# Recommender with GRU and AUGRU: the first 32 pooled features stored and gathered by themselves, and two feature blocks put ahead of the last attention

## The chip, the cores and the metric

The kernel runs on one core of a Trainium2 chip. The metric is the device time of one execution in microseconds (us), as a median over runs. The engines are TensorE (PE, with its weight loads as PEld), VectorE (DVE), ScalarE (ACT), GpSimd (POOL) and SyncE (SP). SP, ACT and POOL issue the DMAs; DMA that gathers rows by an index comes from POOL alone.

## The reference

The model scores 1024 users with a history of 100 items. A GRU runs over the history, an attention network scores each of its states against the candidate item, the scores go through a masked softmax, and the states are pooled with them. Then a second recurrence (AUGRU) runs over the same states, and a small network gives the result.

```python
def gru_step(h, x_t):                                  # 100 steps
    r, z = sigmoid(i_r + h_r), sigmoid(i_z + h_z)
    n = tanh(i_n + r * h_n)
    h_new = (1.0 - z) * n + z * h
keys = swapaxes(gru_seq, 0, 1)
feat = concatenate([keys, q, keys - q, q * keys], axis=-1)
score = mlp(feat, 3 layers, relu)
score = where(mask[:, :, None] == 1, score, -inf)
attn = softmax(score, axis=1)[..., 0]
pooled = einsum('bt,btd->bd', attn, keys)              # 1024 x 128
att_seq = pooled.T[:T]                                 # 100 x 1024

def augru_step(h, (x_t, a_t)):                         # 100 steps
    r = sigmoid([h, x_t] @ aug_Wr.T + aug_br)
    u = sigmoid([h, x_t] @ aug_Wu.T + aug_bu)
    h_hat = tanh([h * r, x_t] @ aug_Wh.T + aug_bh)
    u = a_t[:, None] * u
    h_new = (1.0 - u) * h + u * h_hat
attention_feature = aug_seq at sequential_length - 1
comb = concatenate([user, item, hist_sum, item * hist_sum, attention_feature])
scores = mlp(comb, 3 layers, sigmoid)
```

The weight `a_t` of AUGRU step t is thus feature t of the pooled vector: the first step needs the whole pooling to be done, but of each user only feature 0; step 31 needs feature 31, and the features from 100 on are not used.

## The kernel before, in words

Everything is fp32. The 1024 users lie along the free dimension in two halves of 512 columns, and the 128 features along the partitions. The order of the work is written out by hand: a schedule by hand is kept as it stands in the program, and each engine runs its own instructions in that order. Tiles carry their waits by semaphores.

**GRU steps 0 to 99** (`gru_phase`). A step does, for each half, six products in packed tiles of 128 x 32 weights (line 524), gates on ACT (536, 555, 556) and sums on DVE (544 to 561). The new state is made in a PSUM bank `pi`; DVE multiplies it with the item to `kq` (563), and ACT copies it to SBUF as `hn` (570, `keep`). For half 0 that copy comes after the first gate of half 1, for half 1 in the next step. DVE transposes the state of the step before in blocks of 32 (583) and SP stores it in DRAM as `keys_d`, four steps at a time (597). The attention of a step runs one step later: `attend(t)` on PE (32 packed matmuls, line 688), which needs the banks `pm` of two steps ago to be read; `take(t)` adds the item part on DVE (722) and applies the relu on ACT (727, 729). The layers of the attention network are done as a pipeline over steps, so that `attend(T-1)`, `attend(T)` and `attend(T+1)` remain when the GRU is over. The scores are stored to rows (734), and a softmax over blocks of steps (`ENDS`) runs in `stage`s on DVE (774 to 811) with an exponent on ACT (794). `pool` multiplies states and weights into `pooled` (614 to 625), half 0 on POOL, half 1 partly on DVE.

**The end of the GRU phase** is what the change touches. Six PSUM banks `b[0..5]` are named for what is left: two for the softmax (`e`), one for scratch of the pooling (`kw`), one for scores (`pt`), two for `features` (`f`). `features` are eight blocks of 128 users: the part of the last network that does not need the AUGRU, four inputs by 200 outputs (eight matmuls of 128 x 200, line 655), copied out by ACT (663) and stored by SP a half at a time (665). `some(0, 1)` runs the next part of blocks 0 and 1: called once it issues their matmuls, called again it copies. Between these calls stand the attention steps, the softmax stages, the pooling and `gather_early`, by which POOL fetches key rows for the AUGRU (177). At the end DVE masks the pooled features (967), and they go to DRAM as `pooled_d`, in four parts of 32 features a half: five stores from SP (971), three from ACT (1289).

**The branch.** Three versions of the AUGRU exist, for narrower or wider cuts of the sorted users. Each engine reads which one fits (1342) and branches to it (1343).

**AUGRU** (`augru_phase`). Users are sorted by length, so that the number of columns shrinks over the steps. PE transposes the keys of the first four steps (1070) and ACT copies them (1071); two gates of step 0 are made ahead (1011, 1013). POOL gathers the pooled features in sorted order, 128 users at a time: eight gathers (147) into `att_r`, called `sorted_rows`. Weights for steps 0 and 1 are spread over the partitions by PE (`weight_row`, 1026). For the others, `store_weights` transposes `att_r` on PE (1048), copies it on DVE (1050) and stores it in DRAM (1051), and each step loads its row two steps ahead (`load_att`, 1057). Then come steps 1 to 99, half by half: PE opens the three gates of the next step with its keys (1088) and closes those of this one with the state (1092); ACT applies sigmoid and tanh; DVE does six operations. POOL gathers the key rows of the next block of eight steps, spread over the half-steps (`due`); each gather is preceded by a copy of one column (`pace`, 176), which holds it until DVE's `rest` (1129) of the current half-step.

Of the kernel before, what the change touches and what calls it, by code (L numbers as in the profile page):

```python
# [9 lines left out]
F32 = mybir.dt.float32  # L10
# [9 lines left out]
P = 128  # L20
B = 1024
T = 100
HB = 512
NH = B // HB
NG = B // P
GH = HB // P

R = 32
# [52 lines left out]
def kernel(ctx: ExitStack, tc: tile.TileContext, a: dict, out: bass.AP):  # L81
# [35 lines left out]
    inv_d = dram.tile([B, 2], I32, name="inv_d")  # L117
    over_d = dram.tile([1, 1], I32, name="over_d")
    att_d = [dram.tile([T, HB], F32, name=f"att_d{i}") for i in range(NH)]
    pooled_d = dram.tile([B, P], F32, name="pooled_d")  # L120
    rlen_d = dram.tile([NG, P], F32, name="rlen_d")
    part_d = dram.tile([B, M0], F32, name="part_d")
    early_d = dram.tile([B, 1], F32, name="early_d")
# [32 lines left out]
    def load_rows(q, i, width, tiles):  # L156

        n = READ[q]
        if q < WHOLE:
            r = rows[q, i] = tiles.tile([P, GH, n * P], F32, tag="once", name="rows")  # L160
            for g in range(GH):
                gather(r[:, g, :], keys_d[q], g, i)
                yield
            return

        parts, tag = (2, "kt") if tiles is kx else (1, "rows")
        some = [
            tiles.tile([P, KH // parts, n * R], F32, tag=tag, name="rows") for _ in range(parts)
        ]
        rows[q, i] = some  # L170
        for k in range(-(-width // R)):
            part, at = divmod(k, KH // parts)
            r = some[part]
            if later.get("pace") is not None:

                nc.gpsimd.tensor_copy(r[:, at, 0:1], later["pace"])  # L176
            nc.gpsimd.indirect_dma_start(  # L177
                out=r[:, at, :],
                out_offset=None,
                in_=keys_d[q],  # L180
                in_offset=bass.IndirectOffsetOnAxis(ap=idx_k[:, k, i : i + 1], axis=0),
            )
            yield

    def all_of(steps):
        for _ in steps:
            pass

    def gru_phase(pools):
# [285 lines left out]
        class Half:  # L475
# [37 lines left out]
            def gru(self, t, after_gate, after_sum):  # L513

                x = self.x[t]
                h = self.h[t - 1] if t else hist[:, self.cols]
                hn = hp.tile([P, HB], F32, tag="h", name="hn")
                self.h[t] = hn

                def gate(g, parts):  # L520
                    p = ps.tile([P, HB], F32, tag="g", name=f"ps{g}")
                    for j, (w, v) in enumerate(parts):
                        for q in range(P // R):
                            nc.tensor.matmul(  # L524
                                p[ts(q, R), :],
                                lhsT=w[:, g, ts(q, R)],
                                rhs=v,
                                start=(j == 0),
                                stop=(j == len(parts) - 1),
                            )  # L530
                    return p

                both = ((wih, x), (whh, h)) if t else ((wih, x),)
                pr = gate(0, both)
                r = wp.tile([P, HB], F32, tag="r", name="r")
                nc.scalar.activation(r, pr, AF.Sigmoid, bias=brz[:, 0:1])  # L536
                after_gate()
                if t:
                    ph = gate(2, ((whh, h),))
                pi = gate(2, ((wih, x),))  # L540
                pz = gate(1, both)
                u = wp.tile([P, HB], F32, tag="u", name="u")
                if t:
                    nc.vector.scalar_tensor_tensor(  # L544
                        out=u,
                        in0=ph,
                        scalar=bhh[:, 2:3],
                        in1=r,
                        op0=ALU.add,
                        op1=ALU.mult,  # L550
                    )
                else:
                    nc.vector.tensor_scalar_mul(u, r, bhh[:, 2:3])
                nc.vector.tensor_add(pi, pi, u)  # L554
                nc.scalar.activation(pi, pi, AF.Tanh, bias=bih[:, 2:3])  # L555
                nc.scalar.activation(pz, pz, AF.Sigmoid, bias=brz[:, 1:2])  # L556
                after_sum()
                d = wp.tile([P, HB], F32, tag="d", name="d")
                nc.vector.tensor_sub(d, h, pi)  # L559
                nc.vector.tensor_mul(d, pz, d)  # L560
                nc.vector.tensor_add(pi, pi, d)  # L561
                kq = wp.tile([P, HB], F32, tag="kq", name="kq", bufs=2 * NH)
                nc.vector.tensor_mul(kq, pi, item[:, self.cols])  # L563
                self.first[t] = hn, kq
                self.copy = hn, pi

            def keep(self):

# [334 lines left out]
        all_of(rest)  # L903

        b = [ps.tile([P, HB], F32, tag="g", name="last") for _ in range(6)]
        banks.update(e=[b[0], b[1]], kw=b[3], pt=b[2], f=[b[4], b[5]])

        features = [half.features(g) for half in halves for g in range(GH)]

        def some(*these):  # L910
            for f in these:
                next(features[f])

        gather_early(4)
        halves[1].keep()
        take(T - 2)
        attend(T - 1)
        stage(2)
        weights = soft["e"][0]
        exponents()  # L920
        some(0, 1)
        take(T - 1)
        some(0, 1)
        attend(T)
        some(2)
        for half in halves:
            half.transpose(T - 1)
        stage()
# [8 lines left out]
        halves[1].pool(1, nc.vector)  # L937
        stage()
        take(T)
        some(2)  # L940
        attend(T + 1)
        some(3, 4)
        stage()
        take(T + 1)
        exponents()
        some(3, 4)
        some(5, 6)
        for half in halves:
            half.store((T - 1) // G)
        halves[1].pool(T, nc.vector)  # L950
        stage()
        gather_early(3)
        halves[0].pool(T, nc.gpsimd)
        some(5, 6)
        some(7)
        stage(2)
        exponents()
        some(7)
        stage()
        halves[0].pool(T, nc.gpsimd)  # L960
        halves[1].pool(T, nc.vector)
        all_of(more_early)


        for half in reversed(halves):
            t = blocked(s_bs[NH * (soft["j"] % 2) + half.i])
            nc.vector.tensor_mul(t, later["used"][:, half.ks, :], pooled[:, half.ks, :])
            to = pooled_d[half.cols, :].rearrange("(k r) (p c) -> p r k c", r=R, c=R)
            later["att", half.i] = [(to[p], t[p * R : (p + 1) * R]) for p in range(P // R)]
        for to, t in later["att", 1] + later["att", 0][G - 1 :]:  # L970
            nc.sync.dma_start(out=to, in_=t)

    def augru_phase(pools, widths, alive):
# [43 lines left out]
        def gather_weights(i):  # L1017
            r = wp.tile([P, GH, P], F32, tag="att_r", name="att_r", bufs=2)
            for g in range(GH):
                gather(r[:, g, :], pooled_d, g, i)  # L1020
            return r

        def weight_row(t, i, p):

# [17 lines left out]
            at = att[1, i] = wp.tile([P, HB], F32, name="at", bufs=6)  # L1042
            nc.scalar.copy(at, p)

        def store_weights(i, p):

            for g in range(GH):
                nc.tensor.transpose(p[:, ts(g, P)], sorted_rows[i][:, g, :], ident)
            rows_t = wp.tile([P, HB], F32, tag="att_t", name="att_t", bufs=2)
            nc.vector.tensor_copy(rows_t, p)  # L1050
            nc.sync.dma_start(out=att_d[i], in_=rows_t[:T, :])
            load_att(2, i)

        def load_att(t, i):
            w = widths[t]
# [229 lines left out]
        gates = [first_step(i) for i in range(NH)]  # L1285
        for i in range(NH):
            load_key(1, i, (FREE_BANK, None)[i])
        for to, t in later["att", 0][: G - 1]:
            nc.scalar.dma_start(out=to, in_=t)
        sorted_rows = [gather_weights(i) for i in range(NH)]  # L1290
        for i in range(NH):
            load_key(2, i, (FREE_BANK, None)[i])
        open_gates(1, 1, EARLY_BANKS)
# [5 lines left out]
        first_weights(0, spare)  # L1299
        ahead = load_rows(1, 1, widths[FIRST[1]], kp)  # L1300
        due = spread_over(-(-widths[FIRST[1]] // R), NH * (FIRST[1] - 2))
        jobs, final = [], None
        for t in range(1, T):
            if t + 1 in FIRST[1:-1]:
                all_of(ahead)
                ahead, due = gathers(FIRST.index(t + 1) + 1), spread(FIRST.index(t + 1) + 1)
            for i in range(NH):
                half_step(t, i)
                for _ in range(due.pop(0) if due else 0):
                    next(ahead, None)  # L1310

                for n, job in enumerate(list(jobs)):
                    job[0] += 1
                    if n == 0 and job[0] > 2 * G and next(job[1], job) is job:
                        jobs.remove(job)
            left = alive[t + 1] if t + 1 < T else 0
            for g in range(1, HB // PR):
                if left <= g * PR < alive[t]:
                    jobs.append([0, predict(g)])
                    if left:  # L1320
                        next(jobs[-1][1])
            if t == T - G:
                final = predict(0, last=True)
                next(final)
            if t == HALF_TIME:
                last_places()
# [89 lines left out]
```

## Time and profile before

| what | value |
|---|---|
| median of 3 runs | 2017.64 us (2016.66 to 2018.54) |
| the profiled execution | 2026.01 us |
| its span | 2024.2 us |
| mean granted TensorE clock | 0.994 |
| PE busy | 1995.2 us (99%) |
| DVE busy | 1680.9 us (83%) |
| POOL busy | 1267.8 us (63%) |
| ACT busy | 943.6 us (47%) |
| GRU phase, by the last GRU matmuls | to about 1378 us of the span |
| AUGRU steps 1 to 99 | from about 1433 us of the span to the end |

The profile is of one execution; times in it count from the start of its span. In the page, each row of section 2 cuts the span into 40 slices of 50.6 us. A row of a timeline gives start, duration, engine, line, operation, the tiles and shape, and in brackets how long the engine had been idle before it and what ended that. A table of stretches gives for each the busy time of PE, PEld, DVE, ACT and POOL with the number of instructions, the granted clock, the share of the DMA engines and their rate. Waits, register loads and branches are run by an engine's sequencer; they are marked with a q (PEldq, POOLq) and are not counted as busy.

### The profile page before, as it was taken

The page shows a single profiled execution, that of the slowest core. Times are in us where ns is not written, and L with a number is a line of the kernel's source. Part 1 is how long each engine was busy: PE and PEld are TensorE (multiplying, and loading weights), DVE is VectorE, ACT ScalarE, POOL GpSimd, SP SyncE. Part 2 cuts the span into 40 slices and gives each one's busy share as a digit, 9 for nine tenths or more (in the row PEclk, how much of TensorE's full clock was granted, in tenths as well). Part 3 has the DMA queues.
Part 4 walks back from the last instruction along what each step waited for, and adds up shares of the span by engine and source line. Part 5 has one row for each costly group of instructions (what it writes and reads, how often), then busy time and mean ns, then how long its engine had stood idle before and what let it go on. Part 6 is the DMA issues. An engine that isn't in the chain of part 4 may idle for free.

```text
span 2024.2 us, 41315 instructions
## 1 busy us (share of the span) xinstructions
PE 1995.2 (99%) x15476; PEld 1037.8 (51%) x15476; DVE 1680.9 (83%) x3068; ACT 943.6 (47%) x1708; POOL 1267.8 (63%) x1311
## 2 busy tenths in 40 slices
PE   9999999999999999999999999998999999999998
PEld 2334444444444444444444444444444556678988
DVE  7878998887988887888888888998577777888886
ACT  4444444444445444445444444544334444445555
POOL 0333939569796959595978676998663345453431
PEclk9999999999999999999999999998999999999999
DMA  4443333323344334333432233343443333333332
GB/s 123 97 117 96 101 106 106 105 87 86 105 114 113 106 117 125 100 114 114 123 107 87 84 100 106 91 122 86 132 122 92 92 105 103 97 96 85 92 73 39
DMA packets 241899, 205.81 MB, mean 102 GB/s; under 512 B 59391, under 2 KB 204647, under 8 KB 241687
## 3 DMA queue, kind: packets, MB, share of 16 engines
q1 hardware_dynamic: 227494, 170.04, 30.1%
q0 software_dynamic: 12320, 32.30, 5.7%
q8 instruction: 123, 2.02, 0.4%
q10 hardware_dynamic: 1872, 0.72, 0.1%
q14 instruction: 90, 0.73, 0.1%
HBM read 146.95 MB, written 54.41 MB: 99 GB/s over the span
## 4 chain that ended last, share of the span: by engine, by line
PE 91%; DVE 4%; issue 1%; ACT 1%; POOL 1%; DMA 1%; DVEq 0%; POOLq 0%; ACTq 0%
PE ps L524 48%; PE pm L688 16%; PE ph L1092 5%; PE pr L1092 4%; PE pu L1092 4%; PE ph L1088 4%; PE pr L1088 4%; PE pu L1088 4%; DMA rows<-keys_d,idx_k 1%; POOL pooled L625 0%; POOL kw L624 0%; DVE pu L1116 0%; DVE ps L561 0%; DVE ps L554 0%; DVE d L560 0%
## 5 line engine op out<-in xcount | busy, mean ns | idle before, releaser
L524 PE MATMUL ps<-x,wih 128*32 128x512 f32 x4800 | 723.8, 592 | 0.0
L524 PE MATMUL ps<-hn,whh 128*32 128x512 f32 x4752 | 718.4, 592 | 1.4 <-ACT hn L570 1.4
L524 PEld LDWEIGHTS ps<-x,wih 128*32 128x32 f32 x4800 | 249.7, 110 | 290.1 <-issue 286.9
L524 PEld LDWEIGHTS ps<-hn,whh 128*32 128x32 f32 x4752 | 247.9, 110 | 286.7 <-issue 282.9
L509 POOL TENSOR_TENSOR xm<-x,m 128x512 f32<-128x512 f32 x200 | 234.3, 1172 | 141.7 <-DMA m<-mask_d 141.4
L536 ACT ACTIVATE r<-ps,brz 128x512 f32<-128x512 f32 x200 | 137.5, 687 | 389.2 <-PE ps L524 387.9
L510 POOL TENSOR_TENSOR hist<-hist,xm 128x512 f32<-128x512 f32 x200 | 259.5, 1297 | 15.7
L177 POOL DMA_INDIRECT rows<-keys_d,idx_k x220 | 213.4, 970 | 84.5 <-POOL rows L176 47.6
L625 POOL TENSOR_TENSOR pooled<-pooled,kw 128x512 f32<-128x512 f32 x191 | 245.8, 1287 | 15.0
L624 POOL TENSOR_TENSOR kw<-kt,e 128x512 f32<-128x512 f32 x191 | 205.9, 1078 | 71.0 <-DVE e L797 70.9
L688 PE MATMUL pm<-hn,wk 128*32 128x512 f32 x1200 | 244.6, 594 | 2.2 <-ACT hn L570 2.2
L688 PE MATMUL pm<-kq,wkq 128*32 128x512 f32 x1200 | 244.6, 594 | 0.0
L555 ACT ACTIVATE ps<-ps,bih 128x512 f32<-128x512 f32 x200 | 132.4, 662 | 228.4 <-DVE ps L554 222.6
L1100 ACT ACTIVATE c<-ph,bh 128x96 f32<-128x96 f32 (+41 forms) x198 | 96.4, 487 | 279.3 <-PE ph L1092 247.7
L688 PE MATMUL pm<-mv,w 128*32 128x512 f32 (+1 forms) x808 | 225.2, 596 | 1.0 <-DVE e L778 1.0
L544 DVE SCALAR_TENSOR_TENSOR u<-ps,bhh,r 128x512 f32<-128x512 f32 x198 | 147.5, 745 | 72.4 <-PE ps L524 69.8
L559 DVE TENSOR_TENSOR d<-hn,ps 128x512 f32<-128x512 f32 x198 | 135.9, 687 | 36.0 <-ACT ps L555 35.5
L554 DVE TENSOR_TENSOR ps<-ps,u 128x512 f32<-128x512 f32 x200 | 140.0, 700 | 25.4 <-remote 4.0
L560 DVE TENSOR_TENSOR d<-ps,d 128x512 f32<-128x512 f32 x200 | 138.3, 691 | 26.1 <-ACT ps L556 11.6
L176 POOL COPY rows<-rest 128x1 f32<-128x1 f32 x204 | 38.7, 190 | 192.9 <-DVE rest L1129 189.1
L570 ACT COPY hn<-ps 128x512 f32<-128x512 f32 x200 | 116.5, 582 | 91.9 <-DVE kq L563 91.9
L1116 DVE TENSOR_TENSOR pu<-pu,c 128x96 f32<-128x96 f32 (+41 forms) x197 | 88.1, 447 | 83.7 <-ACT c L1100 73.8
(190 smaller groups left out, 3228.6 us busy)
## 6 DMA issues: line engine op xcount, KB each, us to landing
x<-in_hist_x SPq DMA_DIRECT2D x210, 256.0 KB
keys_d<-kt SPq DMA_DIRECT2D x48, 1024.0 KB
m<-mask_d SPq DMA_DIRECT2D x200, 128.0 KB
rows<-keys_d,idx_k POOLq DMA_INDIRECT x220
s_b<-mv SPq DMA_DIRECT2D x200, 8.0 KB
keys_d<-kt SPq DMA_DIRECT2D x32, 64.0 KB
at<-att_d SPq DMA_DIRECT2D x34, 48.0 KB
mask_i<-in_mask SPq DMA_DIRECT2D x8, 200.0 KB
```

The costliest lines, as they stand in the source:

```text
L177: nc.gpsimd.indirect_dma_start(out=r[:, at, :], out_offset=None, in_=keys_d[q], in_offset=bass.IndirectOffsetOnAxis(ap=idx_k[:, k, i : i + ...
L509: nc.gpsimd.tensor_mul(d, x, m)
L510: nc.gpsimd.tensor_add(acc, acc, d)
L524: nc.tensor.matmul(p[ts(q, R), :], lhsT=w[:, g, ts(q, R)], rhs=v, start=(j == 0), stop=(j == len(parts) - 1),)
L544: nc.vector.scalar_tensor_tensor(out=u, in0=ph, scalar=bhh[:, 2:3], in1=r, op0=ALU.add, op1=ALU.mult,)
L554: nc.vector.tensor_add(pi, pi, u)
L560: nc.vector.tensor_mul(d, pz, d)
L624: eng.tensor_mul(d, k, w)
L625: eng.tensor_add(acc, acc, d)
L688: nc.tensor.matmul(p[i][s, :], lhsT=w[:, s], rhs=v, start=start, stop=stop)
L1088: nc.tensor.matmul(p, lhsT=m[:, 1, :], rhs=k, start=True, stop=False)
L1092: nc.tensor.matmul(p, lhsT=m[:, 0, :], rhs=v, start=False, stop=True)
```

## The change

The tensor `pooled_d` becomes two: features 0 to 31, and the others. Of each half the first 32 features are stored from SP right after the mask of that half; the other three parts of half 1 follow on SP, those of half 0 on ACT. Ahead of the AUGRU, POOL gathers only the first 32 features. The others are gathered one a half-step from step 5 on (eight gathers, each with a copy for the pace), and transposed and stored as weights of steps 32 to 99 in step 12. The last two key-row gathers of `rows[1, 0]` move from the end of the GRU phase to behind the gathers of weights. In the list of the last attention, feature blocks 0 and 1 come ahead of `take(T - 2)` and `attend(T - 1)`, and the other blocks each move up; the six banks are given out in another order. In the last GRU step the copy of half 1's state comes ahead of `kq` and no longer after it.

```diff
-    pooled_d = dram.tile([B, P], F32, name="pooled_d")
+    pooled_d = [
+        dram.tile([B, n], F32, name=f"pooled_d{j}") for j, n in enumerate((R, P - R))
+    ]
...
+                self.copy = hn, pi
+                if t == T - 1 and self.i:
+                    self.keep()
                 kq = wp.tile([P, HB], F32, tag="kq", name="kq", bufs=2 * NH)
                 nc.vector.tensor_mul(kq, pi, item[:, self.cols])
                 self.first[t] = hn, kq
-                self.copy = hn, pi
...
-        banks.update(e=[b[0], b[1]], kw=b[3], pt=b[2], f=[b[4], b[5]])
+        banks.update(e=[b[0], b[5]], kw=b[4], pt=b[3], f=[b[1], b[2]])
...
         gather_early(4)
-        halves[1].keep()
+        some(0, 1)
         take(T - 2)
         attend(T - 1)
         stage(2)
         weights = soft["e"][0]
         exponents()
         some(0, 1)
+        some(2, 3)
         take(T - 1)
-        some(0, 1)
+        some(2, 3)
         attend(T)
-        some(2)
+        some(4)
...
         take(T)
-        some(2)
+        some(4)
         attend(T + 1)
-        some(3, 4)
+        some(5, 6)
         stage()
         take(T + 1)
         exponents()
-        some(3, 4)
         some(5, 6)
+        some(7)
         for half in halves:
             half.store((T - 1) // G)
         halves[1].pool(T, nc.vector)
         stage()
         gather_early(3)
         halves[0].pool(T, nc.gpsimd)
-        some(5, 6)
         some(7)
         stage(2)
         exponents()
-        some(7)
         stage()
         halves[0].pool(T, nc.gpsimd)
         halves[1].pool(T, nc.vector)
-        all_of(more_early)
+        gather_early(3)
...
-            to = pooled_d[half.cols, :].rearrange("(k r) (p c) -> p r k c", r=R, c=R)
-            later["att", half.i] = [(to[p], t[p * R : (p + 1) * R]) for p in range(P // R)]
-        for to, t in later["att", 1] + later["att", 0][G - 1 :]:
+            first, others = (
+                d[half.cols, :].rearrange("(k r) (p c) -> p r k c", r=R, c=R) for d in pooled_d
+            )
+            nc.sync.dma_start(out=first[0], in_=t[:R])
+            later["att", half.i] = [
+                (others[p - 1], t[p * R : (p + 1) * R]) for p in range(1, P // R)
+            ]
+        for to, t in later["att", 1]:
             nc.sync.dma_start(out=to, in_=t)
...
-                gather(r[:, g, :], pooled_d, g, i)
+                gather(r[:, g, :R], pooled_d[0], g, i)
             return r
+
+        def gather_more():
+            for i in range(NH):
+                for g in range(GH):
+                    r = sorted_rows[i][:, g, R:]
+                    nc.gpsimd.tensor_copy(r[:, 0:1], later["pace"])
+                    gather(r, pooled_d[1], g, i)
+                    yield
...
-        def store_weights(i, p):
-
+        def store_weights(i, p, t0=0, t1=R):
+
+            n = t1 - t0
             for g in range(GH):
-                nc.tensor.transpose(p[:, ts(g, P)], sorted_rows[i][:, g, :], ident)
+                nc.tensor.transpose(p[:n, ts(g, P)], sorted_rows[i][:, g, t0:t1], ident)
             rows_t = wp.tile([P, HB], F32, tag="att_t", name="att_t", bufs=2)
-            nc.vector.tensor_copy(rows_t, p)
-            nc.sync.dma_start(out=att_d[i], in_=rows_t[:T, :])
-            load_att(2, i)
+            nc.vector.tensor_copy(rows_t[:n, :], p[:n, :])
+            nc.sync.dma_start(out=att_d[i][t0:t1], in_=rows_t[:n, :])
+            if t0 == 0:
+                load_att(2, i)
...
-        for to, t in later["att", 0][: G - 1]:
+        for to, t in later["att", 0]:
             nc.scalar.dma_start(out=to, in_=t)
         sorted_rows = [gather_weights(i) for i in range(NH)]
+        for k in range(14, KH):
+            load_row(1, 0, k)
...
+        more = gather_more()
...
             for i in range(NH):
                 half_step(t, i)
                 for _ in range(due.pop(0) if due else 0):
                     next(ahead, None)
+                if t > FIRST[1]:
+                    next(more, None)
+                if t == FIRST[2]:
+                    store_weights(i, pa.tile([P, HB], F32, tag="a", name="pw"), R, T)
```

`FIRST[1]` is 4 and `FIRST[2]` is 12, `R` is 32, `KH` is 16. `load_row(q, i, k)` is the body of the loop in `load_rows`, as a function of its own.

More of the change, by code (lines that the diff above doesn't have):

```diff
@@ L171, in load_rows, with load_row @@
         for k in range(-(-width // R)):
[L172 to L182, printed above, removed]
-            yield
+            load_row(q, i, k)
+            yield
+    def load_row(q, i, k):
+        some = rows[q, i]
+        part, at = divmod(k, KH // len(some))
+        r = some[part]
+        if later.get("pace") is not None:
+            nc.gpsimd.tensor_copy(r[:, at, 0:1], later["pace"])
+        nc.gpsimd.indirect_dma_start(
+            out=r[:, at, :],
+            out_offset=None,
+            in_=keys_d[q],
+            in_offset=bass.IndirectOffsetOnAxis(ap=idx_k[:, k, i : i + 1], axis=0),
+        )
     def all_of(steps):
@@ L967, in gru_phase @@
             nc.vector.tensor_mul(t, later["used"][:, half.ks, :], pooled[:, half.ks, :])
-            to = pooled_d[half.cols, :].rearrange("(k r) (p c) -> p r k c", r=R, c=R)
-            later["att", half.i] = [(to[p], t[p * R : (p + 1) * R]) for p in range(P // R)]
-        for to, t in later["att", 1] + later["att", 0][G - 1 :]:
+            first, others = (
+                d[half.cols, :].rearrange("(k r) (p c) -> p r k c", r=R, c=R) for d in pooled_d
+            )
+            nc.sync.dma_start(out=first[0], in_=t[:R])
[3 more added lines that the diff above has]
+        for to, t in later["att", 1]:
             nc.sync.dma_start(out=to, in_=t)
```

## The prediction

> **What bounds the kernel now.** I read the page first, then the busy time of each engine in stretches of 10 us, then, at the one place where TensorE (PE) is not full, the timeline of each engine and the chain of waits.
>
> ```profile
> span 2024.2 us, 41315 instructions
> PE 1995.2 (99%) x15476; PEld 1037.8 (51%) x15476; DVE 1680.9 (83%) x3068; ACT 943.6 (47%) x1708; POOL 1267.8 (63%) x1311
> PE   9999999999999999999999999998999999999998
> ```
>
> PE carries the time in both recurrences. The dip is slice 28, where the attention ends and the AUGRU starts. Only there can earlier work shorten the run; after it every microsecond that PE starts earlier stays won, since PE is full again to the end.
>
> ```profile
> 1370.00:1380.00 10.00, 8.38 (x77) 4.42 (x69) 9.09 (x15) 3.91 (x8) 9.69 (x9) 1.00 0.01 2
> 1380.00:1390.00 10.00, 9.43 (x52) 6.12 (x54) 6.34 (x16) 5.06 (x9) 6.22 (x7) 0.83 0.20 57
> 1390.00:1400.00 10.00, 9.14 (x47) 6.09 (x44) 9.48 (x20) 3.62 (x8) 9.01 (x9) 1.00 0.12 33
> 1400.00:1410.00 10.00, 4.51 (x24) 3.96 (x23) 9.04 (x27) 1.16 (x5) 8.84 (x9) 0.90 1.01 306
> ...
> 1420.00:1430.00 10.00, 6.71 (x25) 3.38 (x24) 0.00 (x0) 2.31 (x4) 4.98 (x6) 0.92 0.27 58
> 1430.00:1440.00 10.00, 9.34 (x33) 5.97 (x34) 5.44 (x9) 2.64 (x5) 2.62 (x3) 0.74 0.17 47
> 1440.00:1450.00 10.00, 10.00 (x34) 5.13 (x33) 7.24 (x12) 3.86 (x6) 7.62 (x14) 1.00 0.54 154
> ```
>
> Columns: PE, PEld, DVE, ACT, POOL busy, granted clock, DMA share, GB/s. From 1387 to 1415 DVE and POOL are full (the last softmax and pooling) and PE has holes; from 1420 DVE is empty and waits for PE. The clock is down in three places. PE's timeline there:
>
> ```profile
> 1380.57 1.06 PE L688 MATMUL pm<-hn,wk 128*32 128x512 f32 x2 [2.19 <-ACT hn L570]
> ...
> 1408.19 1.94 PE L1070 MATMUL pk<-ident,rows 128*128 128x128 f32 x8 [5.49 <-issue]
> ...
> 1427.21 0.71 PE L1026 MATMUL first<-ident,att_r 128*128 128x128 f32 x4 [0.72 <-issue]
> 1429.83 1.23 PE L1026 MATMUL first<-ident,att_r 128*128 128x128 f32 x4 [1.91 <-issue]
> ```
>
> Three holes: 2.19 us before the attention of the last GRU step, 5.49 us before the first AUGRU key, 1.91 us in the first attention weight. The instructions of two lines explain the second and third:
>
> ```profile
> L1343 PEldq COMPARE_BRANCH  x1: 6799/6799/6799, 1401.2 to 1401.2; - x1
> L1343 ACTq COMPARE_BRANCH  x1: 50/50/50, 1405.2 to 1405.2; - x1
> ```
> ```profile
> L147 POOLq EVENT_SEMAPHORE  x4: 43/43/4689, 1417.8 to 1422.7; - x4
> ```
>
> PE stands 6.8 us in the branch to the AUGRU's code while DMA is full (share 1.01: two stores of the last keys). ACT branches at 1405.2 and copies the first key at 1409.98. POOL waits 4.69 us, to 1422.5, for the eight stores of the pooled features, of which the last left ACT's queue only at 1420.0. So the gathers of weights start at 1423.49, one each 1.26 us.
>
> **The change part by part**, against the profiled execution (2026.01 us, of them 2024.2 us span; 8.4 us over the median of the runs shown; I carry the difference over to the median).
>
> *Feature blocks 0 and 1 ahead of the last attention.* Two blocks are 16 matmuls, 1386.41 to 1389.31, 2.9 us. They now fill the hole: PE goes on from 1377.7 to 1380.6. Here a rule speaks against a gain. The Trainium skill, "TensorE: Matmul & The Clock Gate", section "Why this matters for your kernels", asks for "No PE-idle gaps >~3µs between matmul bursts", so 2.19 us would cost only itself, and as the data are not ready before, nothing is won. The trace shows otherwise: after the 2.19 us the clock is 0.50 to 1384.0, and the 32 matmuls take 6.57 us, where those of earlier steps take 3.43. I use the trace. The same page says, under "What's actually happening", that the window is free-running, so not each execution need have this drop; the sum below allows for that.
>
> *The copy of the last state (L570) ahead of kq (L563).* In all 200 cases the copy waits for kq, which only reads the same bank (91.9 us of idle, ended by kq), so the two are kept apart. Turned round, DVE's kq waits for the 0.58 us copy, and behind it on DVE the two sums f (L722), which ACT's relus and the attention need: +0.6 us. The relus then end at 1381.7 and 1382.3; 28 matmuls at 0.107 us and 0.5 us of drain follow: 1385.9, where DVE had waited to 1387.23. So DVE and POOL are 1.25 us earlier from here, to the end of the pooling.
>
> *The other blocks, each two places earlier.* Block 2 now waits for ACT's copy of block 0, which is behind table load and exponent (1.6 us after DVE's last softmax step, now 1384.5): 1386.5. Blocks 2 and 3 end at 1389.4, so the next attention starts as before (1389.31): nothing won on PE, nothing lost, as the scores were early (no wait of DVE for them). Block 7 follows block 6 at 1397.4 instead of 1401.2. PE branches some 3 us earlier. SP's store of part features no longer holds up the key stores, which go 1.9 us earlier: DMA stays as full around the branch, so I leave its 6.8 us: PE ready at 1405, first transposes 1406.
> ACT's branch hangs on the last exponent (DVE): 1404.0, 1.25 us earlier. From branch to first copy it took 4.7 us under full DMA. With full DMA again the copy is 1.3 us earlier; with free DMA, as POOL shows (branch 1412.8, next request 1415.5: 2.7 us), 3.3 us. The stores run out by about 1407, so I take the middle, 2.3 us. From there to the first weight, 17.2 us of transposes, first gates and copies, mostly PE and ACT in turn, stay. PE is ready for it at 1424.9 instead of 1427.2.
>
> *Stores and gathers.* Only two stores (SP, one a half) are waited for, issued at 1413.1 and 1413.7. The last old store took 2.5 us from its issue's end; with 3 us the wait ends at 1417. All of POOL's own work ahead is now three row gathers instead of five (2.5 us less; they end at 1415.8). Gathers of weights then start about 1417.5, the fourth at 1421.3; landing (2.4 us in the chain, up to 3.2 beside the other stores) by 1424.5. Both are under PE's 1424.9, so the 1.91 us hole closes. Two row gathers (2.5 us) come behind the weights on POOL; POOL then idles 6.95 us before step 1 today, which hides them. The three remaining ACT stores wait for DVE's end (1413.6), ACT gets there at 1416.
> Sum at the second four of the first weight: 1429.83 becomes 1424.9 + 0.45 = 1425.35: -4.5 us.
>
> *Clock after that.* The hole at 1428 brought 0.50 to 1435. Undisturbed, the chain from 1429.83 to the second half's first gate (1438.73) is 2.0 us shorter (0.6 in the first weights, 1.0 in the reset gate, 0.4 in the next). Transposes with small holes come before, and may still drop the clock: 0 to -2.0, taken -1.0.
>
> *In the AUGRU.* Step 1 transposes 32 rows instead of 128 features: same instructions. Step 12 adds 8 transposes on PE, 0.44 us for four in the chain: +0.9 us, not hidden, as PE is full. Its two DVE copies (0.69 us) lie in DVE's slack (7.5 of 10 us busy; PE reaches ph 1.5 us after r is ready). SP gets two more stores with the loads of steps 14 behind them, which have two steps (20 us). POOL gets 8 pairs of copy and gather in steps 5 to 8 (1.44 us each: 0.19 + 0.97 + gaps), behind row gathers; bound: 0 if the rows are still in time, see the slow rival.
>
> Sum: -4.5 - 1.0 + 0.9 = -4.6 us; in executions in which the first drop was not there the kernel before is up to 1.75 us faster; if that is half of them it is 0.9 us on average, and as only part of it reaches the key chain I carry +0.4: **-4.2 us, 2013.4 us**. The ends of the unknown terms (ACT 1.3 to 3.3, clock 0 to 2, drop 0 to 1.75) give -1.5 to -6.6.
>
> **The rivals.**
> *The key chain stays where it was (little or no gain).* ACT's branch still takes as long under full DMA, kq's wait eats the DVE gain, and only the hole in the weights closes: -2.2 - 0.5 (clock) + 0.9 = -1.8: 2015.8 us. For it: DVE gains only 1.25 us, and where the clock did not drop before, DVE is 0.5 us later than before. Against it: the features leave PE 3.7 us earlier and the 4.69 us wait is shown. If the gather still waited for all stores (the change not doing what it says), it would end here or at 2017; two separate tensors speak against that.
>
> *POOL falls behind (slower).* Place: steps 5 to 8, POOL's queue. The rows of steps 12 to 19 (30 gathers) are spread over the 12 half-steps of steps 3 to 8 and are transposed by DVE in step 10, where a late one stops DVE, then PE. A half-step is 5.1 us; 2.5 pairs become 3.5, 5.04 us at 1.44: just in. 38 pairs have 14 half-steps, 71 us; it decides from 1.88 us a pair. At 2.1 us the last row is 9 us late: 2017.6 - 4.2 + 9 = 2022.4. For it: more gathers beside full stores land later, and each waits for an earlier landing. Against: POOL's 38 us of idle waiting for DVE's rest between 1440 and 1560, and transposes waited 0.6 us for rows in the whole run.
>
> **How the numbers follow.** What a measurement of this kernel can tell from no change is about 0.2%, 4.0 us: below 2013.6 or above 2021.7. The forecast 0.57, with nearly all of its earlier half and the larger clock gains below 2013.6; the key-chain rival 0.31, POOL 0.12. A few hundredths of the first lie above 2013.6, as much of the second below it: faster 0.56, within 0.32, slower 0.12. Range: from 2009.0 (all unknown terms at their good end, -6.6, and 2 us for the branch gone) to 2018.0 (rival one with the kq wait and no clock gain, and noise); beyond are POOL and some hundredths.
>
> **What would show it.** Right: no hole before the last attention and clock 1.00 there; first key copy near 1407.7; first gather of weights near 1417.5; no 1.91 us hole; PE full in steps 3 to 20 with 0.9 us more of transposes in step 12. Wrong: the last attention ends after 1387; ACT's first key copy stays at 1410; a new hole of PE where DVE's key transposes wait for rows in step 10; gathers of weights still after 1422.

## The result and the profile after

The changed kernel takes 2012.61 us in the median of 15 runs (2011.05 to 2014.81), the kernel before 2016.66 us beside it (15 runs, 2014.58 to 2018.54). The ratio is 0.998, 95% interval 0.9973 to 0.9987: 4.05 us less. The profiled execution of the changed kernel took 2013.1 us. The page of the changed kernel:

```profile
span 2011.3 us, 41368 instructions
...
PE 1989.6 (99%) x15484; PEld 1008.0 (50%) x15484; DVE 1683.1 (84%) x3070; ACT 943.9 (47%) x1708; POOL 1275.5 (63%) x1327
...
PE   9999999999999999999999999998999999999998
```

The two spans differ by 12.9 us, three times the medians. So the spans must not be subtracted: 8.3 us of the difference lie in AUGRU steps 50 to 99, where the two kernels issue the same work. I therefore count from one event that both have, the end of the last GRU sum on DVE. The changed kernel gets there at 1379.81 us of its span, the one before at 1379.10; 0.71 us are taken off when times of the two are compared.

Its busy time in stretches (PE, PEld, DVE, ACT, POOL, granted clock, DMA share, GB/s):

```profile
1370.00:1380.00 10.00, 10.00 (x88) 3.95 (x81) 8.93 (x14) 4.65 (x9) 9.69 (x9) 1.00 0.01 2
1380.00:1390.00 10.00, 9.48 (x60) 6.03 (x58) 7.68 (x18) 5.26 (x10) 7.26 (x8) 1.00 0.20 57
...
1400.00:1410.00 10.00, 2.63 (x9) 2.07 (x10) 9.01 (x28) 2.06 (x5) 8.85 (x9) 0.68 0.83 252
1410.00:1420.00 10.00, 9.29 (x28) 3.99 (x26) 4.30 (x7) 4.87 (x9) 6.71 (x7) 0.81 0.47 90
1420.00:1430.00 10.00, 7.79 (x34) 4.70 (x35) 1.39 (x2) 2.30 (x5) 7.60 (x8) 1.00 0.14 21
1430.00:1440.00 10.00, 9.34 (x41) 5.18 (x40) 7.45 (x12) 3.91 (x6) 4.32 (x7) 1.00 0.39 111
```

Two of the three places with a low clock are gone, 1380 to 1390 and the one after the first weight (1428 to 1435 in the kernel before). The one around the branch has stayed. PE's timeline at the former holes, and the branch:

```profile
1381.91 1.05 PE L696 MATMUL pm<-hn,wk 128*32 128x512 f32 x4
...
1387.21 0.61 PE L663 MATMUL last<-m,user 128*128 128x200 f32 x2 [0.52 <-ACT part L671]
...
1405.51 1.94 PE L1092 MATMUL pk<-ident,rows 128*128 128x128 f32 x8 [5.84 <-issue]
...
1420.13 1.12 PE L1110 MATMUL pu<-k,wu 128*128 128x510 f32 x2 [0.40 <-ACT k L1093]
...
1426.30 1.16 PE L1046 MATMUL first<-ident,att_r 128*128 128x128 f32 x8 [0.72 <-ACT k L1093]
```
```profile
L1372 PEldq COMPARE_BRANCH  x1: 6606/6606/6606, 1398.7 to 1398.7; - x1
L1372 ACTq COMPARE_BRANCH  x1: 50/50/50, 1404.8 to 1404.8; - x1
```

The attention at 1381.91 has no wait before it. The first weight runs as one group of eight at 1426.30; the hole of 1.91 us between its fours is closed. The 6.6 us in the branch remain, only earlier. ACT and POOL in the changed kernel:

```profile
1416.80 2.66 ACTq L1311 DMA_DIRECT2D pooled_d<-s_b  x3
1419.50 1.06 ACT L1093 COPY k<-pk 128x506 f32<-128x506 f32 x2 [2.19 <-DMA pooled_d<-s_b]
```
```profile
1418.79 0.95 POOL L149 DMA_INDIRECT att_r<-pooled_d,idx  x1 [2.20 <-DMA pooled_d<-s_b]
```

The gathers start at 1418.79. The issue of ACT's three remaining stores takes 2.66 us and holds back the next key copy, for which PE waits 0.40 us at 1420.13.

### The profile page after: what moved, and what is told of

It is laid out like the page before. It is cut to its first block, busy times and chain, and to the rows that moved or that the text cites. A ratio compares the mean times of both kernels' runs of the same rounds, so it can differ in the third digit from the quotient of the medians.

```text
span 2011.3 us, 41368 instructions
## 1 busy us (share of the span) xinstructions
PE 1989.6 (99%) x15484; PEld 1008.0 (50%) x15484; DVE 1683.1 (84%) x3070; ACT 943.9 (47%) x1708; POOL 1275.5 (63%) x1327
## 3 DMA queue, kind: packets, MB, share of 16 engines
q8 instruction: 124, 2.03, 0.4%
## 4 chain that ended last, share of the span: by engine, by line
PE 96%; DVE 2%; issue 1%; ACT 1%; DMA 0%; ACTq 0%; DVEq 0%
PE ps L530 49%; PE pm L696 17%; PE ph L1114 5%; PE pr L1114 5%; PE pu L1110 5%; PE pu L1114 5%; PE ph L1110 5%; PE pr L1110 5%; PE p L1205 0%; PE p L1233 0%; PE p L1200 0%; PE pd L239 0%; DVE ps L560 0%; DVE ps L567 0%; DVE d L566 0%
## 5 line engine op out<-in xcount | busy, mean ns | idle before, releaser
L530 PE MATMUL ps<-x,wih 128*32 128x512 f32 x4800 | 617.7, 593 | 0.0
L530 PE MATMUL ps<-hn,whh 128*32 128x512 f32 x4752 | 611.3, 592 | 0.9 <-ACT hn L578 0.9
L530 PEld LDWEIGHTS ps<-x,wih 128*32 128x32 f32 x4800 | 218.0, 110 | 300.9 <-issue 297.6
L530 PEld LDWEIGHTS ps<-hn,whh 128*32 128x32 f32 x4752 | 216.2, 110 | 296.7 <-issue 293.5
L696 PE MATMUL pm<-hn,wk 128*32 128x512 f32 x1200 | 222.1, 592 | 0.0
L696 PE MATMUL pm<-kq,wkq 128*32 128x512 f32 x1200 | 222.0, 592 | 0.0
L696 PE MATMUL pm<-mv,w 128*32 128x512 f32 (+1 forms) x808 | 195.4, 592 | 0.6 <-DVE e L786 0.6
```

The source lines that it names most:

```text
L530: nc.tensor.matmul(p[ts(q, R), :], lhsT=w[:, g, ts(q, R)], rhs=v, start=(j == 0), stop=(j == len(parts) - 1),)
L696: nc.tensor.matmul(p[i][s, :], lhsT=w[:, s], rhs=v, start=start, stop=stop)
```

## The experiments

The runs were made in two lots, each on one chip with the kernel before beside it: 2014.67 us in the median on the first chip, 2022.23 on the second. Only kernels of one lot are compared by their times. Between lots I use stages, each read from one profile, in us after the end of the last GRU sum on DVE. "Sums f" are DVE's sums behind the attention of the last GRU step; the first weight is the attention weight of step 0, made by PE in two groups of four; the last two rows are where ACT starts the reset gate, of step 1's second half and of step 13.

| stage | before | before again | features only | split only | keys first | changed | changed again |
|---|---|---|---|---|---|---|---|
| sums f of the last attention | 8.13 | 6.37 | 6.98 | 6.36 | 6.37 | 6.98 | 8.03 |
| PE starts its branch | 22.13 | 20.34 | 19.11 | 20.34 | 18.31 | 18.92 | 20.09 |
| first key copy on ACT | 30.88 | 29.13 | 28.47 | 29.13 | 27.65 | 28.37 | 29.68 |
| first gather of weights | 44.39 | 42.49 | 42.85 | 38.03 | 38.10 | 38.98 | 39.77 |
| first weight begins | 48.11 | 46.20 | 45.71 | 46.77 | 45.61 | 46.49 | 48.05 |
| its second four | 50.72 | 48.20 | 48.71 | 47.32 | 46.16 | 47.03 | 48.60 |
| step 1, second half | 60.85 | 58.65 | 58.79 | 55.56 | 54.34 | 55.22 | 58.94 |
| step 13 | 173.50 | 171.30 | 171.49 | 169.08 | 167.93 | 168.81 | 172.53 |

**The features alone** (`e1_features_only`). The kernel before, with the new order of the last attention, the early copy and the banks, and with the old stores and gathers.

```diff
+                if t == T - 1 and self.i:
+                    self.keep()
...
-        halves[1].keep()
+        some(0, 1)
         take(T - 2)
         attend(T - 1)
...
```

> The kernel before with the new order of feature blocks, the new banks and the early copy of the last state, but one tensor of pooled features, all eight stores waited for and the gathers as before. Theory (the two parts add up, and the wait for the stores ends last): only the 1.15 us by which DVE and POOL are earlier reaches the first weight, so -1.2 us (about 2015.5 us where before is 2016.7), and the hole of PE in the first weight grows from 1.9 to over 2.5 us, because the key chain arrives earlier. Rival (the feature blocks carry the gain): -3 to -4 us. Rival (the feature blocks are hidden anyway): 0.

Measured: 2014.09 us, ratio 0.9998 (0.9989 to 1.0007). In the stages it is 0.2 us behind the kernel before of the same lot ("before again") at step 13. PE branches 1.2 us earlier and reaches the first weight 0.5 us earlier, and there it waits for the gathers, which start 0.4 us later than they did. PE's timeline of this kernel, and the one row of before again that has a hole in the first weight:

```profile
1425.01 0.49 PE L1027 MATMUL first<-ident,att_r 128*128 128x128 f32 x2 [0.48 <-DMA att_r<-pooled_d,idx]
...
1427.05 1.24 PE L1027 MATMUL first<-ident,att_r 128*128 128x128 f32 x4 [1.55 <-DMA att_r<-pooled_d,idx]
```
```profile
1426.84 1.42 PE L1026 MATMUL first<-ident,att_r 128*128 128x128 f32 x4 [1.29 <-DMA att_r<-pooled_d,idx]
```

What the key chain (from the branch over the first key copy to the first weight) wins, the holes in the weight give back: two of 2.03 us together, where before again has 1.29. The 1.2 us expected did not arrive.

**The split alone** (`e2_split_only`). The changed kernel, with the old order of the last attention.

```diff
-        some(0, 1)
+        halves[1].keep()
         take(T - 2)
         attend(T - 1)
...
```

> The changed kernel with the feature blocks, the banks and the copy of the last state as before: only the split of stores and gathers and the moved row gathers. Theory: the hole in the first weight closes (-2.2 us), the clock does not drop there (-1 to -1.8 us), step 12 costs +0.9 us: -2.3 to -3.1 us (about 2014 us); where the clock drops at the last attention it drops here too. Rival (without the earlier key chain the split gains nothing): over -1 us. Rival (the split is all): -4 us.

Measured: 2011.65 us, ratio 0.9986 (0.9977 to 0.9995), 3.0 us less than before. The gathers start 4.5 us earlier, the hole (1.29 us in this lot) is closed, and step 13 is 2.2 us earlier than in before again, with the 0.9 us of step 12 in it. The first weight itself begins 0.6 us later; the gain lies behind it, where the clock no longer drops. This part carries most of the gain.

**Keys ahead of the copy** (`e3_kq_first`). The changed kernel, but the item product `kq` comes first again, and the copy behind it; the features still stand ahead of the attention.

```diff
-                self.copy = hn, pi
-                if t == T - 1 and self.i:
-                    self.keep()
...
+                self.copy = hn, pi
...
+        halves[1].keep()
         some(0, 1)
```

> The changed kernel with kq ahead of the copy of the last state, as it was. Theory: DVE does not wait 0.65 us for the copy, so the last attention, the exponents and ACT's branch are 0.6 us earlier and the kernel 0.3 to 0.6 us faster than the changed one (-4.5 us against before). Rival (the key chain hangs on DMA at the branch, not on DVE): the same as the changed kernel, -4.0 us, and no hole of 0.65 us on DVE in the profile.

Measured: 2010.15 us, ratio 0.9981 (0.9972 to 0.999), the fastest kernel of this lot: 1.5 us below the split alone, by its medians. First the changed kernel's DVE, then that of this one:

```profile
1380.46 0.69 DVE L572 TENSOR_TENSOR kq<-ps,item 128x512 f32<-128x512 f32 x1 [0.65 <-ACT hn L578]
```
```profile
1377.81 0.69 DVE L569 TENSOR_TENSOR kq<-ps,item 128x512 f32<-128x512 f32 x1
```

The wait of 0.65 us is gone, and the sums f come 0.61 us earlier. At step 13 the lead is 0.9 us; the rest came mainly where ACT's three stores held PE up for 0.31 us less than in the changed kernel, which need not be due to the edit. So the features bring something (1.15 us at step 13 against the split alone), and in these profiles the early copy took most of it away again. The changed kernel was not in this lot; that keys first beats it is read from one profile each, and not shown in times side by side. On the second chip it does not show at all (see the changed kernel again).

**The kernel before again** (`e4_before_again`).

> The kernel before once more, for a second profile. Theory: the 8 us by which the first profiled execution was over the median lie in steps 50 to 99 and belong to that execution: here the time is 2014 to 2019 us and from step 20 to the end it takes as long as the changed kernel, within 1 us; whether the clock drops at the last attention is open. Rival: those steps are really slower in the kernel before, and the 8 us come again.

Measured: 2014.81 us, span 2012.7 us, 11.5 us shorter than the first profile of the same kernel. Its late AUGRU has the pace of the changed kernel. And its hole before the last attention is there, without the drop of the clock that followed it in the first profile; PE's timeline and the stretch:

```profile
1380.11 1.05 PE L688 MATMUL pm<-hn,wk 128*32 128x512 f32 x4 [2.23 <-ACT hn L570]
```
```profile
1380.00:1390.00 10.00, 9.89 (x58) 5.20 (x59) 8.08 (x17) 4.90 (x9) 7.94 (x8) 1.00 0.20 57
```

The drop was there in one of three profiles with that hole (before; before again and the split alone have none). By PE's records the last attention ends 1.12 us later with it (7.38 us after the last GRU sum and 6.26). The sums f come 1.76 us later (8.13 and 6.37): in the first profile they began 0.76 us after PE's modelled end, here 0.11. So 0.6 us of this are not shown to be the clock's; the changed kernel again has the same sign. At step 13 the two profiles are 2.2 us apart.

**The three stores of ACT on SP** (`e5_stores_sp`), in the kernel with keys first.

```diff
         for to, t in later["att", 0]:
-            nc.scalar.dma_start(out=to, in_=t)
+            nc.sync.dma_start(out=to, in_=t)
```

> The kernel with kq first, and the three stores of the other features of half 0 from SP instead of ACT. Theory (the ACT queue is held by these stores: they take 2.35 us there and the next key copy comes 1.9 us late, which leaves PE a hole of 0.3 to 0.4 us before the last of the first gates): the hole goes, the first weight comes 0.3 to 0.5 us earlier, the whole is 0.3 us faster than with kq first. Rival (the key copy waits for DMA, not for the queue, or SP's stores now delay something): no change or slower by up to 1 us.

Measured: 2021.49 us, ratio 0.9996 (0.9987 to 1.0005), beside the changed kernel's 0.9999 on the same chip; these two can't be told apart. ACT's hold is gone:

```profile
1420.17 0.58 ACT L1092 COPY k<-pk 128x506 f32<-128x506 f32 x1 [0.27 <-issue]
```

The stretch from first key copy to first weight takes 18.1 us here (1409.61 to 1427.74) and 18.4 in the changed kernel of the same lot (29.68 to 48.05). This 0.25 us is the sum of two things. Where the stores had held PE, from the first opening gate to the first weight, it is 0.57 us shorter (7.77 and 8.34, the same 7.8 as in the kernel before). Ahead of that it is 0.32 us longer: the low clock around the branch lasts 13.7 us here and 10.2 there. So the forecast gain is there in its stage (0.3 to 0.5 us), and too small to be seen in the times.

**An extra product to keep the clock** (`e6_warm`), in the kernel with keys first; `WARM` is 1.

```diff
+        warm = bank("warm", EARLY_BANKS[-1])
+        for _ in range(WARM):
+            nc.tensor.matmul(warm, lhsT=item[:, :P], rhs=item[:, :HB], start=True, stop=True)
```

> The kernel with kq first, and one more fp32 matmul of 128 x 512, whose result nobody reads, behind PE's first key transposes, where PE stands 1.8 us at half clock and waits for ACT. Theory (a stretch of transposes and waiting does not lift the clock, a stretch of matmuls does): the clock is back up to 3.4 us earlier, the four products of step 0 take up to 1.7 us less, and the first weight and the whole are 1.0 to 1.7 us faster than with kq first, if the gathered weights are there (the fourth lands 44.3 us after the GRU's last sum, so not all of it counts). Rival (the clock there does not hang on what PE does in this wait, or the matmul comes in the way): 0, or up to 2 us slower.

Measured: 2025.56 us, ratio 1.0018 (1.0009 to 1.0027). The longer time says nothing on the clock:

```profile
1413.78 2.08 PE L1309 MATMUL warm<-item 128*128 128x512 f32 x2 [6.03 <-DVE pooled L632]
```

The bank I took is the pooling's scratch, in use until DVE ends, so PE waited 6.03 us. What lifts the clock here, and whether an earlier lift would help, was not tried otherwise and stays open.

**POOL's work doubled** (`e7_pool_twice`): every pair of copy and gather of the other features is done twice.

```diff
+                    nc.gpsimd.tensor_copy(r[:, 0:1], later["pace"])
+                    gather(r, pooled_d[1], g, i)
```

> The changed kernel with each of the eight gathers of the other features, and its copy for the pace, done twice in steps 5 to 8, so that POOL has 46 pairs instead of 38 in steps 3 to 9. Theory (POOL has room: the key rows are needed only in step 10): no change against the changed kernel within 0.3 us from step 3 to step 13. Rival (POOL is at its limit there): DVE's key transposes of step 10 wait for rows, PE shows a hole, and it is 4 to 11 us slower.

Measured: 2045.59 us, ratio 1.0117 (1.0102 to 1.0133). It loses 21.7 us on the changed kernel in steps 8 to 12 (22.6 less 0.9, both against the pace of the kernel before), and nothing after. The waits of DVE, and then POOL's copies:

```profile
DVE rest L1153 <- POOL att_r L1041: 29.0, 6, 5.5
```
```profile
L1041 POOL COPY att_r<-rest x8: 182/183/183, 1485.5 to 1547.1; 128x1 f32<-128x1 f32 x8
its engine sat idle before it (us, times) until:
  DMA att_r<-pooled_d,idx: 17.6, 8
who waited for it (us, times):
  DVE rest L1153: 29.0, 6
```

This is not a clean doubling: the second copy overwrites the tile of the first gather and waits for its landing, 2.2 us each (17.6 over 8). But it shows how a late POOL would hurt. POOL's pace copies read DVE's `rest`; when they lag, DVE finds no free buffer for a new `rest` (29.0 us in six waits). The key rows of step 10, where my slow rival had put the stall, count for little: the whole wait of DVE's key transposes for them was 1.0 us.

**The changed kernel again** (`e8_after_again`), on the second chip.

> The changed kernel once more, on the same chip as the others. Theory: -2.5 us against executions of the kernel before whose clock does not drop at the last attention, -4.7 us against those where it does, so -2.5 to -4.5 us in the median; e3 stays 0.9 us ahead of it. Rival: -4 us whatever the chip.

Measured: 2021.35 us, ratio 0.9999 (0.999 to 1.0008). On this chip the gain is not there. The gathers start at 39.77 us and the hole is closed, as before; but the sums f are 1.05 us later than in its first profile, and the reset gate of step 1's second half starts 3.7 us later (58.94 against 55.22). DVE's first sum f of this profile and of the kernel with its stores on SP; then ACT's copy of the first spread weight, in the first profile and in this one:

```profile
1386.50 1.29 DVE L730 TENSOR_TENSOR f<-pm,q 128x512 f32<-128x512 f32 x2 [2.62 <-PE pm L696]
```
```profile
1388.14 1.29 DVE L728 TENSOR_TENSOR f<-pm,q 128x512 f32<-128x512 f32 x2 [3.27 <-remote]
```
```profile
1428.39 0.59 ACT L1063 COPY at<-spare 128x512 f32<-128x512 f32 x1 [2.14 <-PE spare L1046]
```
```profile
1432.41 0.59 ACT L1063 COPY at<-spare 128x512 f32<-128x512 f32 x1 [5.94 <-PE pw L1069]
```

By its record the last product into `spare` ended 1428.58 us in the second, 3.8 us before the copy, so ACT got the end of PE's work late, or it waited for something that the profile does not show. The same stands in two of the other three profiles of this chip (4.0 us each; 0.3 in the extra product's). So the stretch from the weight's second four to step 1's second half takes 10.3 us here and not 8.2: the 1.9 us or more that the split won there in the other profiles are missing.

It is alike at the sums f. In all four profiles of this chip they begin 8.00 to 8.08 us after the last GRU sum, with the copy early or not, although PE's attention ends at 6.26 us with keys first and at 6.87 with the early copy. What they wait for is thus not PE's last product as recorded, and the order of copy and keys makes no difference at this place. The late AUGRU (steps 50 to 99) is 4.7 us longer than in the changed kernel's first profile; the excess sits in single half-steps: 9 to 10 of them are over 0.2 us longer than the shortest on record, against 2 in the five profiles of before again, the first lot's other kernels and the changed kernel.

The first profile of the kernel before has the same signs: its sums f are 0.76 us late, and it has 14 such half-steps, most of them at the same steps. So part of what sets it apart from the changed kernel's profile is no property of the kernel. The kernel before was not profiled again on this chip. Why the handing over is late here, and whether that alone takes the gain away, stays open.

## Why the prediction was right, step by step

The forecast of 2013.4 us was off by 0.8 us, and the measured time is in its range. The parts that it named did move: gathers, hole, branch and clock. The size of the sum is right in part by luck, as the end of this section says. Times in this part are in the count of the kernel before (0.71 us off).

- *Features in the hole.* As forecast: no wait, clock 1.00, f 1.15 us earlier than in the first profile (forecast 1.25). But against the kernel before without its clock drop, the sums f are 0.61 us later (6.98 against 6.37), the price forecast for the early copy (0.6). Without the drop the features pay only by PE's earlier branch. The price of the drop was read too high: the 6.57 us that the forecast took are those of the chain of waits, up to DVE's sums; by PE's own records its 32 matmuls took 5.91 us (to 1386.48), against 4.79 in before again. And the copy, which always stood behind kq, waited for it in 113 of the 200 cases, not in all.
- *Later blocks.* PE waits 0.52 us for ACT's copy before block 2, and blocks 2 and 3 end at 1389.5 (forecast 1389.4).
- *Branch and key chain.* PE branches 3.2 us earlier (forecast some 3), its branch is as long (6.6 us), and ACT's first copy comes at 1407.48, 2.5 us earlier (forecast 2.3).
- *The term mis-sized.* From that copy to the first weight I let the 17.2 us stay; it took 18.1 us. So PE was ready at 1425.6, 1.6 us earlier and not 2.3. Most of the 0.9 us (0.67) came where PE opens the gates of step 1, 8.45 us to the first weight and not 7.78: ACT's three stores took 2.66 us (before 1.59), and the key copy behind them came too late for PE. I had put this hold at no change. Another 0.30 us came in the four products of step 0 (5.82 us, before 5.52): the low clock around the branch lasted 10.2 us in the changed kernel, 6.8 in the one before, so more of them ran at half speed. The transposes between took 0.09 us less.
- *Stores and gathers.* First gather 1418.08 (forecast 1417.5), hole closed. The second four came 3.7 us earlier (forecast 4.5).
- *The clock after the hole.* Mis-sized the other way: the stretch from the second four to step 1's second half shrank from 10.13 to 8.19 us, 1.94 us (forecast 1.0), as the drop that followed the hole is gone: it stands in all three profiles without the split, and in none of the seven with it. In the kernel before again that stretch took 10.45 us, so this gain does not depend on the chance drop at the last attention.
- *AUGRU.* Step 12 cost 0.88 us (forecast 0.9). The transposes of the changed kernel, and POOL's work from 1475 to 1530 us (first its groups, then its waits):

```profile
L1069 PE MATMUL pw<-ident,att_r x12: 272/272/273, 1430.9 to 1546.8; 128*68 128x128 f32 x8, 128*32 128x128 f32 x4
```
```profile
L149 POOL DMA_INDIRECT att_r<-pooled_d,idx x8 | 7.8, 969 | 2.2 <-POOL att_r L1039 2.2
...
L1039 POOL COPY att_r<-rest 128x1 f32<-128x1 f32 x8 | 1.5, 193 | 0.0
```
```profile
POOL rows L183 <- DVE rest L1151: 1.7, 1, 1.7
```

A pair takes 1.44 us (0.97, 0.27 and 0.19) as forecast, and POOL has next to no idle left in this window: one wait of 1.7 us for DVE's `rest`. It was close, but DVE waited for no copy of POOL in these steps, once for key rows to land (0.9 us), and PE for none of it.

The sum at step 13 is then -3.7 - 1.9 + 0.9 = -4.7 us, where the forecast had -4.5 - 1.0 + 0.9 = -4.6: two errors, 0.8 us too much in the key chain and 0.9 us too little in the clock, all but cancelled. And of the 3.7 us, 2.5 set the first profile of the kernel before apart from its second. Against that second one the terms are -1.17, -2.26 and +0.94, together -2.5 us: the key chain wins far less than forecast, and the clock behind the hole carries the gain. My +0.4 us for executions without the first drop was too small for a single one. Nor does the bad end of -1.5 us follow from its terms: -4.6 + 1.0 + 1.0, with the 0.8 us of the drop that I let reach the key chain, gives -1.8, and with its whole 1.75 us -0.9.

The first chip of the experiments, with its 3.0 us for the split alone and 4.5 for keys first, agrees with the mechanism; the second, with 0.9 us or nothing, was not foreseen by any case of mine.

Of the rivals, POOL falling behind did not happen. "The key chain stays" describes, without the first drop, about the right size (-1.8 forecast, -2.5 measured), though by another way: the key copy did move, 0.8 us against the kernel before again.

## What to carry to other kernels

When work is waited for through one store queue, split the tensor so that the first consumer waits for its own small part, and pay the rest where the consumer is later: here that part alone closed a hole of 1.3 to 1.9 us and spared the clock drop behind it, for 0.9 us of added work in step 12. On the first chip, where it was run alone, it was worth 3.0 us; on the second the whole change showed no gain. Filling a hole with independent work is worth only what the next wait lets through: alone it brought nothing, after the split 1.15 us. Ask of each reordering that comes with such a change whether it is needed: the early copy was not, and cost 0.6 us at the sums behind it on the first chip. And take a second profile of the same kernel before a difference of two profiles is put down to a change: here two of one kernel lay 2.2 us apart at step 13.

## What was unexpected of the hardware

- The same hole of 2.2 us on PE was followed by half clock in one execution and by full clock in two others; PE's attention ended 1.1 us later. A single profile of the kernel before had shown the worse case. All low periods ahead of the end of the span, in ten traces, last 3.41 us or two, three or four times that, as if the clock were set in steps of 3.41 us. Counted back from the low periods of each trace, the hole of the first profile has 2.18 us of idle PE in one such step; in before again at most 2.01 us fall in one, in the split alone 1.72. This is an estimate from three cases. The Trainium skill, "TensorE: Matmul & The Clock Gate", section "What's actually happening", calls the window free-running, which fits one hole with two outcomes.
- PE's branch took 6.3 to 6.9 us in all ten profiles, wherever it stood.
- DVE's sums f began 0.11 us after PE's modelled end in five profiles and 0.8 to 1.8 us after it in five others; where late, they stood at 8.00 to 8.13 us, whenever PE ended.
- One program differed by 7.6 us in its median between the two chips (2014.67 and 2022.23), and kernels with the split won 3.0 and 4.5 us on the first, 0.7 and 0.9 us, not to be told from nothing, on the second (each with other small edits).
